# A vision tower's last three blocks: two routings at other places in the ending, and the last Exp in another method

## The chip, the cores and the metric

The kernel runs on one core of a Trainium2 chip. Its time is the device time of one execution in microseconds (us), and the median over several runs counts. The engines are TensorE (PE: matmuls; its weight loads are listed as PEld), VectorE (DVE), ScalarE (ACT) and GpSimd (POOL). SyncE (SP) issues most of the DMAs; ACT and POOL issue some from their own queues.

## The reference

A tokenizer, one layer with a recurrence ("retention") and an MLP, and a mixture of eight experts with the best two taken for each token, all in float32. Cut to what matters:

```python
# tokens: 16 samples of every 8, rfft over them, projected to D = 256
h = x_emb.reshape(B, V * N, -1)                  # 32 * 512 rows in all, 256 wide
# layer, on _layernorm(h)
q, k, v = n @ Wq.T + bq, n @ Wk.T + bk, n @ Wv.T + bv     # n = layernorm of the input
mem = decay * mem + k_t * v_t ;  ret_t = q_t * mem        # a scan over the tokens
x = x + ret
x = x + relu(layernorm(x) @ W1.T + b1) @ W2.T + b2        # W1: 1024 x 256
h = h + x
# experts, on tokens = layernorm(h)
logits = tokens @ router_w.T                              # 8 experts
rw, re = top_k(softmax(logits), 2);  rw = rw / rw.sum()
out = tokens + sum over e of combine[:, e] * (gelu(tokens @ w1[e] + b1[e]) @ w2[e] + b2[e])
h = h + out
```

## The kernel before

The 16,384 tokens are worked on in 32 blocks of 512 (`NB` = 32, the last is `NS` = 31), each as four tiles of 128 tokens on the partitions. Everything is fp32. A block passes through these steps, each a method of `Block`; the lines are those of the profile:

- `embed`: the tokenizer's products (L396) and its norm.
- `first_norm`, `retention` or `qkv` and `scan`: q, k, v from the transposed tokens (L339 on `wqkv_sb` in the ending), then on DVE `kv` L476, the scan `ks` L484 and `ret` L494. ACT makes a first `ks` (L474) and `z` (L438).
- `residual`: `ret` is turned back to tokens on PE (L608), added on DVE (L611) and normalized: statistics L263 and L264, a reciprocal square root by some ten small instructions L271 to L277, and `zz` L292.
- `features1`, `features2`: transposes of `zz` by DMA or on PE (L305), copied from PSUM on ACT (L306).
- `mlp_in(m)`, eight of them: one eighth of the first MLP product (L339 on `w1_sb`, `hT`), with relu on ACT (`aT`, L640). `mlp_out(u)`: the second product (L650, 32 matmuls each), added on DVE (L657), and after the second the norm that gives `tok` (L292).
- `rows`, `turn3`, `join3`, or `features3`: the tokens as rows in memory (ACT L698), and transposed for the router. `turn3` sends them through four transposing DMAs (L326, issued by SP) and `join3` puts the halves together (L332, on DVE for block 29); `features3` uses PE (L305) and ACT (L306).
- `logits` (PE L723), `choose` (DVE L747 to L764, then `ex`), `place` (PE L796, DVE L798 to L807, `weights` L774 to L777, then eight indirect DMAs of POOL, L819, which scatter the block's rows to `xbuf`, sorted by expert).
- `take(n, block, writes)` (DVE L864 to L932) plans the expert tiles: 256 rows of one expert each. `FULL` fixes how many tiles there are after each block. Block 29 gives four tiles, block 30 eighteen.

An expert tile (`Tile`) is handled in six steps. `load` (SP): weights `w` of 641.5 KB (L965), the rows transposed `xh` (L972) and their numbers `xg` (L975). `fetch` (L989): where `w` isn't loaded, it is copied from `bank`, on DVE and ACT in turn. `turn`: ACT makes `xT` (L995). `enter`: PE's first product (L1002) and gelu on ACT (L1010). `leave`: PE's second product (L1019). `sums`: DVE's L1031 to L1043, then two indirect DMAs of POOL which add the rows to `out` (L1048). `expert_halves` does one tile's enter and leave together with the other steps of the tiles ahead of it; `expert_step` runs it through. `bank` holds all eight experts' weights; `load_bank` issues its eight loads of 641.5 KB on ACT's queue (L944), one at each `next(weights)`. Before, only the tiles of block 30 take `w` from it. The last block isn't scattered: `combine` makes a weight for each token and expert, and `Expert` (PE L1081 and L1098, ACT L1088, DVE L1106 and L1112) computes all eight experts for its 512 tokens, between the tiles of block 30.

On SP, PE, DVE and ACT the order of the source is the order on the engine (`manual_schedule`); POOL's is left to a scheduler. So the order is written out by hand in a loop over blocks 0 to 30, in which three blocks are at work, and in an ending for the last three, called `old` (29), `mid` (30) and `last` (31). Pools bound how far an engine runs ahead: five `w`, six `xh`, twelve `xg`, four `y`, two `xT` and two `ge` buffers, and in PSUM two `mm` (for L305, L1002 and L1081) and three `tm` (for L608, L650, L723, L1019 and others).

Of the kernel before, what the change touches and what calls it, by code (L numbers as in the profile page):

```python
# [36 lines left out]
def vit_tower_kernel(  # L37
# [15 lines left out]
    nc = tc.nc  # L53
# [196 lines left out]
    def restore_weights():  # L250

        w = wqkv_sb.rearrange("p w k (m q) -> p w k m q", q=P)
        nc.vector.tensor_tensor(w[:, :, 0, 1], w[:, :, 1, 1], w[:, :, 0, 1], ALU.subtract)
# [96 lines left out]
    class Block:  # L350
# [381 lines left out]
        def choose(self):  # L732

            ps = self.lg
            shape = [P, TT, E]

            def wide(a):
                return a.unsqueeze(2).to_broadcast(shape)

            lg = small.tile(shape, F32, name="lg")  # L740
            top = small.tile([P, TT], F32, name="top")
            if self.i == NS:
                first_key = small.tile([P, TT], F32, name="first_key")
            else:
                first_key = self.row.bitcast(F32)[:, :, FIRST]
            turned = small.tile([P, TT, G], F32, name="turned_lg")
            nc.vector.transpose(turned.rearrange("p t g -> p (t g)"), ps.rearrange("p t g -> p (t g)"))  # L747
            nc.vector.tensor_reduce(top, turned[:, :, :E], AX.X, ALU.max)
            nc.vector.tensor_tensor(lg, turned[:, :, :E], wide(top), ALU.subtract)
            key = small.tile(shape, F32, name="key")  # L750
            self.oh = oh = small.tile([P, 2, TT, E], F32, name="oh")
            nc.vector.scalar_tensor_tensor(key, lg, 0.0, key0, ALU.is_equal, ALU.mult)
            nc.vector.tensor_reduce(first_key, key, AX.X, ALU.max)
            nc.vector.tensor_tensor(oh[:, 0], key, wide(first_key), ALU.is_equal)
            nc.vector.scalar_tensor_tensor(lg, oh[:, 0], -3.0e38, lg, ALU.mult, ALU.add)
            second = small.tile([P, TT], F32, name="second")
            nc.vector.tensor_reduce(second, lg, AX.X, ALU.max)
            nc.vector.tensor_tensor(key, lg, wide(second), ALU.is_equal)
            nc.vector.tensor_tensor(key, key, key0, ALU.mult)
            nc.vector.tensor_reduce(top, key, AX.X, ALU.max)  # L760
            nc.vector.tensor_tensor(oh[:, 1], key, wide(top), ALU.is_equal)
            dtype = F32 if self.i == NS else BF16
            self.both = small.tile(shape, dtype, name=f"both_{dtype.name}")
            nc.vector.tensor_tensor(self.both, oh[:, 0], oh[:, 1], ALU.add)  # L764
            self.ex = small.tile([P, TT], F32, name="ex")
            if self.i == NS:
                nc.scalar.activation(self.ex, second, AF.Exp)
            else:
                nc.gpsimd.tensor_tensor(self.ex, euler, second, ALU.pow)

# [7 lines left out]

        def combine(self):

            diff = small.tile([P, TT], F32, name="diff")
            second = small.tile([P, TT], F32, name="second")
            self.weights(diff, second)
            shape = [P, TT, E]
            self.share = self.both
            nc.vector.tensor_tensor(self.share, self.both, second.unsqueeze(2).to_broadcast(shape), ALU.mult)
            first = self.oh[:, 0]
            nc.vector.tensor_tensor(first, first, diff.unsqueeze(2).to_broadcast(shape), ALU.mult)
            nc.vector.tensor_tensor(self.share, self.share, first, ALU.add)
# [68 lines left out]
    def take(n, block, writes):  # L858
# [40 lines left out]
        expert = small.tile([P, KMAX], F32, name="expert")[:, :k]  # L899
        nc.vector.tensor_reduce(expert, past, AX.X, ALU.add)  # L900
        table = four.tile([P, 2, KMAX], I32, name="table")[:, :, :k]
        if block.i >= NS - 1:
            nc.vector.tensor_scalar(table[:, 0, :], expert, float(E - 1), None, ALU.min)
        else:
            nc.vector.tensor_scalar(table[:, 0, :], expert, float(P), float((E - 1) * P), ALU.mult, ALU.min)
# [47 lines left out]
    class Tile:  # L953
# [6 lines left out]
        def load(self):  # L960
            t = self.t
            self.w = five.tile([P, NW], F32, name="w")
            if self.block.i < NS - 1:
                wrow = nc.sync.value_load(self.table[:, 0, t : t + 1], min_val=0, max_val=(E - 1) * P)
                nc.sync.dma_start(out=self.w, in_=wex[bass.ds(wrow, P), :])  # L965

            def rows():
                row = nc.sync.value_load(self.table[:, 1, t : t + 1], min_val=0, max_val=ROWS - S)
                return xbuf[bass.ds(row, S), :]

            self.xh = six.tile([P, 2 * KD, S], U16, name="xh")
            read = nc.sync.dma_start(out=self.xh, in_=rows().bitcast(U16)[:, : 2 * D], transpose=True)  # L972
            unordered("rows", read, self.writes)
            self.xg = twelve.tile([P, 2, RW - D], I32, name="xg")
            read = nc.sync.dma_start(out=self.xg, in_=rows()[:, D:].rearrange("(c p) d -> p c d", p=P))  # L975
            unordered("rows", read, self.writes)
# [3 lines left out]
            return self.block.put == TT  # L980

        def fetch(self):
            if self.block.i >= NS - 1:

                assert len(loaded) == E
                t = self.t
                engine, copy = ((nc.vector, nc.vector.tensor_copy), (nc.scalar, nc.scalar.copy))[t % 2]
                e = engine.value_load(self.table[:, 0, t : t + 1], min_val=0, max_val=E - 1)
                copy(self.w.unsqueeze(1), bank[0][:, bass.ds(e, 1), :])  # L989
# [135 lines left out]
    def advance(what, upto):  # L1125
        while at[what] < min(upto, len(tiles)):
            if what == "load" and not tiles[at[what]].there():
                break
            getattr(tiles[at[what]], what)()
            at[what] += 1  # L1130

    def expert_halves(fetch=True, sums=True, load=True, turn=True):

        n = at["enter"]
        if load:
            advance("load", n + AHEAD)
        assert at["load"] >= min(n + 2, len(tiles))
        advance("turn", n + 1 + turn)
        advance("enter", n + 1)
        yield  # L1140
        advance("leave", n)
        if sums:
            advance("sums", n)
        if fetch:
            advance("fetch", n + AHEAD)

    def run(steps):
        for _ in steps:
            pass

    def expert_step(**how):
        run(expert_halves(**how))
# [2 lines left out]

    LEFT = 3

    def slot_halves(known, load=True, sums=True):

        if len(tiles) - at["enter"] > LEFT and at["enter"] + 2 <= known:  # L1160
            yield from expert_halves(load=load, sums=sums)

    def slot(known, load=True):
# [8 lines left out]
    with tc.manual_schedule(engines=MANUAL):  # L1172
# [3 lines left out]
        for i in range(NS):  # L1176
# [54 lines left out]
            if i:  # L1231
# [16 lines left out]
                    old.scatter(2, last_product[0])  # L1248
                next(qkv)
                advance("sums", at["leave"])  # L1250
                later = slot_halves(known, load=False)
                next(later, None)
                next(qkv)
                new.first_norm()
# [45 lines left out]
        old.join3(nc.vector.tensor_copy)  # L1300
        for m in range(KH):
            mid.mlp_in(m)
            if m in (1, 3, 5, 7):
                next(weights)
            if m == TT - 1:
                expert_step()
            if m == KH - 3:
                last.features1()
        next(weights)
        old.logits()  # L1310
        old.choose()
        expert_step()
        writes = old.place()
        next(weights)
        restore_weights()
        last.first_norm()
        last.retention(0)
        mid.mlp_out(0)
        next(weights)
        take(NS - 1, old, writes)  # L1320
        next(weights)
        mid.mlp_out(1)
        last.retention(1)
        beside = expert_halves(fetch=False)
        next(beside)
        mid.features3()
        mid.rows()
        advance("leave", at["enter"] - 1)
        mid.logits()
        mid.choose()  # L1330
        run(beside)
        expert_step(fetch=False, sums=False)
        writes = mid.place()
        advance("sums", at["leave"])
        expert_step(fetch=False, sums=False)
        last.residual()
        expert_step(fetch=False, sums=False)
        advance("sums", at["leave"])
        expert_step(fetch=False)
        take(NS, mid, writes)  # L1340

        last.features2()
        expert_step(turn=False)
        mid.store()
        last.sum_up()
        for m in range(KH):
            last.mlp_in(m)
            if m == TT - 1:
                advance("turn", at["enter"] + 1)
            if m == KH - 3:  # L1350
                expert_step()
# [109 lines left out]
```

## Time and profile before

| | us |
|---|---|
| median of five runs | 2114.7 |
| lowest and highest of them | 2111.08, 2118.17 |
| the profiled execution | 2115.45 |
| its span, first to last instruction | 2113.7 |
| PE busy in the span | 2080.0 |
| DVE busy | 1674.4 |
| ACT busy | 1099.6 |
| POOL busy | 885.0 |
| granted clock of PE, mean of the span | 0.994 of full |

A line of the timeline gives the start in us from the span's start, the duration, engine, source line, operation, output and inputs, and the number of instructions of the group; in brackets stand the idle time of the engine ahead of it and what ended that ("issue": nothing that the profile shows). In the waits of an engine a line names the waiting line, the releaser, the total in us, the number and the longest. In the table of windows each engine has its busy time and number of instructions in a stretch, then follow the granted PE clock, the DMA share and GB/s.

The ending begins near 1855 us of the span. In it stand, in this order, the first MLP product of block 30 (from 1862.8), block 29's router (L723 at 1880.94), the first q, k, v of the last block, both halves of `mlp_out` (from 1890.53), the second q, k, v, block 30's router (L723 at 1915.58), residual (L608 at 1923.30), the MLP of the last block with tiles between its parts, and from 2000 us on the experts.

### The profile page before, as it was taken

What the parts mean: (1) busy time and instruction counts of PE and PEld (TensorE: products, weight loads), DVE (VectorE), ACT (ScalarE), POOL (GpSimd) and SP (SyncE); (2) the same over time, 40 slices, a digit from 0 to 9 for tenths busy, and PEclk for the clock granted to TensorE, in tenths of its full rate; (3) what the DMA queues carried; (4) which work ended last, traced back from release to release, by engine and by line L of the source; (5) the groups of instructions that cost most, each with busy time, mean ns of one, the idle gap of its engine ahead of it and who ended that gap; (6) DMA issues with size and microseconds to landing.
All of it is one profiled execution on the core that took longest, in us unless ns stands there. A gap on an engine that the chain in (4) does not pass through costs nothing.

```text
span 2113.7 us, 30454 instructions
## 1 busy us (share of the span) xinstructions
PE 2080.0 (98%) x9042; PEld 1577.6 (75%) x9042; DVE 1674.4 (79%) x5179; ACT 1099.6 (52%) x1966; POOL 885.0 (42%) x768
## 2 busy tenths in 40 slices
PE   8999999999999999999999999999999999998999
PEld 6777677777777777777777777787777787675776
DVE  6778888888888888888888888888888888767445
ACT  2344455655545665555556555455665545544443
POOL 1032234444444444444444444444444444534444
PEclk9999999999999999999999999999999999999999
DMA  4031256766676676667667766676776667686553
GB/s 142 2 123 64 80 135 139 160 142 122 140 157 147 157 159 137 130 138 160 153 148 160 149 124 137 157 155 144 163 159 122 132 150 161 141 224 141 90 70 49
DMA packets 424519, 283.21 MB, mean 134 GB/s; under 512 B 355104, under 2 KB 391072, under 8 KB 420256
## 3 DMA queue, kind: packets, MB, share of 16 engines
q1 hardware_dynamic: 373424, 208.35, 42.4%
q0 software_dynamic: 49632, 67.39, 17.5%
q10 hardware_dynamic: 1296, 5.52, 0.7%
q8 instruction: 71, 1.16, 0.2%
q14 instruction: 96, 0.79, 0.1%
HBM read 118.36 MB, written 86.52 MB: 97 GB/s over the span
## 4 chain that ended last, share of the span: by engine, by line
PE 75%; DVE 10%; DMA 5%; ACT 5%; issue 2%; SPq 2%; POOL 1%; ACTq 0%; DVEq 0%; POOLq 0%
PE tm L650 17%; PE sums L339 14%; PE tm L396 9%; PE sums L524 9%; PE mm L1002 9%; PE tm L1019 8%; DMA turned<-planes 3%; DVE st L263 2%; SPq L326 2%; PE mm L540 1%; ACT planes L318 1%; PE tm L1098 1%; PE mm L1081 1%; PE mm L539 1%; ACT tokT L332 1%
## 5 line engine op out<-in xcount | busy, mean ns | idle before, releaser
L1048 POOL DMA_INDIRECT out<-y,xg x226 | 365.7, 1618 | 426.4 <-DVE y L1038 220.4
L650 PE MATMUL tm<-w_sb,aT 128*128 128x256 f32 x2048 | 454.7, 380 | 0.0
L339 PE MATMUL sums<-hT,w_sb 128*128 128x512 f32 x1024 | 451.1, 593 | 0.3 <-ACT aT L640 0.3
L650 PEld LDWEIGHTS tm<-w_sb,aT 128*128 128x128 f32 x2048 | 386.7, 190 | 57.2 <-DVE z L611 4.9
L819 POOL DMA_INDIRECT xbuf<-row,to x248 | 258.8, 1044 | 293.9 <-DVE ks L560 170.6
L339 PEld LDWEIGHTS sums<-hT,w_sb 128*128 128x128 f32 x1024 | 193.5, 190 | 218.2 <-issue 200.9
L396 PE MATMUL tm<-wu,xv 128*128 128x256 f32 x1280 | 282.5, 379 | 0.0
L318 ACT COPY planes<-zz 128x1024 uint16<-128x1024 uint16 x100 | 99.3, 1040 | 342.1 <-DVE zz L292 342.1
L396 PEld LDWEIGHTS tm<-wu,xv 128*128 128x128 f32 x1280 | 242.7, 190 | 32.7
L1002 PE MATMUL mm<-xT,w 128*128 128x256 f32 x1048 | 252.3, 384 | 5.2 <-ACT xT L995 3.4
L1019 PE MATMUL tm<-w,ge 128*128 128x256 f32 x1048 | 253.9, 385 | 0.0
L1002 PEld LDWEIGHTS mm<-xT,w 128*128 128x128 f32 x1048 | 201.1, 193 | 47.9 <-issue 15.6
L1019 PEld LDWEIGHTS tm<-w,ge 128*128 128x128 f32 x1048 | 196.5, 191 | 31.7 <-issue 2.9
L640 ACT ACTIVATE aT<-sums,vec 128x512 f32<-128x512 f32 x256 | 166.9, 691 | 59.8 <-PE sums L339 57.8
L995 ACT COPY xT<-xh 128x512 uint16<-128x512 uint16 x262 | 182.1, 767 | 20.2 <-DMA xh<-xbuf 17.2
L1010 ACT ACTIVATE ge<-mm,w 128x256 f32<-128x256 f32 x262 | 109.7, 474 | 140.6 <-PE mm L1002 84.7
L283 POOL TENSOR_SCALAR rstd<-mv 128x4 f32<-128x4 f32 x62 | 41.9, 676 | 333.2 <-DVE mv L264 296.7
L1036 DVE TENSOR_TENSOR y<-tm,w 128x512 f32<-128x512 f32 x131 | 90.5, 691 | 99.0 <-PE tm L1019 98.5
L332 ACT COPY hT<-turned 128x512 uint16<-128x512 uint16 x100 | 66.2, 761 | 80.4 <-DMA turned<-planes 80.4
L263 DVE BATCH_NORM_STATS2 st<-h 128x6 f32<-128x256 f32 x256 | 104.9, 410 | 3.3
L524 PE MATMUL sums<-hT,wqkv_sb 128*128 128x256 f32 x360 | 107.1, 379 | 0.0
L371 DVE TENSOR_TENSOR xv<-xb 128x512 f32<-128x512 f32 x160 | 104.3, 684 | 3.5 <-DMA xb<-in_x 3.5
(224 smaller groups left out, 3081.0 us busy)
## 6 DMA issues: line engine op xcount, KB each, us to landing
w<-in_wex SPq DMA_DIRECT2D x113, 641.5 KB
xb<-in_x SPq DMA_DIRECT2D x32, 1040.0 KB
out<-h SPq DMA_DIRECT2D x31, 512.0 KB
bank<-in_wex ACTq DMA_DIRECT2D x8, 641.5 KB
xbuf<-row,to POOLq DMA_INDIRECT x248
out<-y,xg POOLq DMA_INDIRECT x226
xh<-xbuf SPq DMA_TRANSPOSE x131
xg<-xbuf SPq DMA_DIRECT2D x131, 4.0 KB
```

Of the source, the lines that this page charges most:

```text
L263: nc.vector.bn_stats(self.st[:, t, :], src[:, t, :])
L318: nc.scalar.copy(planes[:, :, i * D : (i + 1) * D], half)
L339: nc.tensor.matmul(ps, lhsT=w[:, k, ts(m, P)], rhs=rhs[:, k, :], start=k == 0, stop=k == KD - 1)
L396: nc.tensor.matmul(ps[:, n, :], lhsT=xv[:, i, j, :], rhs=wu[:, i, j, :], start=j == 0, stop=j == J - 1)
L524: nc.tensor.matmul(g[:, n, :], lhsT=lhsT, rhs=rhs, start=False, stop=True, skip_group_check=True)
L640: nc.scalar.activation(self.aT[:, m, :], ps, AF.Relu, bias=vec[:, MB1 + m : MB1 + m + 1])
L650: last_product[0] = nc.tensor.matmul(ps[:, i, :], lhsT=self.aT[:, k, ts(u * 2 + i, P)], rhs=w2_sb[:, k, :], start=k == 0, stop=k == KH - 1,)
L819: write = nc.gpsimd.indirect_dma_start(out=xbuf, out_offset=bass.IndirectOffsetOnAxis(ap=self.to[:, c, t : t + 1], axis=0), in_=self.row[: ...
L995: nc.scalar.copy(halves[:, :, :, 1 - i], self.xh[:, i * KD : (i + 1) * KD, :])
L1002: nc.tensor.matmul(ps[:, m, :], lhsT=self.w[:, k * D + m * P : k * D + (m + 1) * P], rhs=self.xT[:, k, :], start=k == 0, stop=k == KD - 1,)
L1019: last_product[0] = nc.tensor.matmul(ps[:, c, :], lhsT=self.ge[:, k, ts(c, P)], rhs=w[:, (2 + k) * D : (3 + k) * D], start=k == 0, stop=k ...
L1048: add = nc.gpsimd.indirect_dma_start(out=out, out_offset=bass.IndirectOffsetOnAxis(ap=number[:, c, :], axis=0), in_=y[:, c, :], in_offset= ...
```

## The change

Four things are edited.

- The last block's Exp is called in `combine` instead of `choose`.
- The tiles of block 29 take `w` from `bank` as those of block 30 do: three conditions on `NS - 1` become `NS - 2`, in `take` (the table then holds the number of an expert instead of a row), `load` and `fetch`.
- The ending is put in another order. Block 29's `logits` and `choose` come inside block 30's first MLP product, after m = 4, and its `place` right after m = 7; two expert steps there are gone from their places. Both halves of `mlp_out` of block 30 come next, with block 29's `take` between them, and the first q, k, v product of the last block after them. Block 30's router follows with one tile and a half around it, then its `place`, `take(NS)`, the second q, k, v product, two expert steps, `residual`, two expert steps and `features2`. Block 30's store and the last block's `sum_up` come after m = 1 of the last `mlp_in`, and the expert step which skips a `turn` after m = 3. `restore_weights` and the bank's loads are at other places.
- `slot_halves` takes a parameter `left` whose value is everywhere the constant that was there.

```diff
             if self.i == NS:
-                nc.scalar.activation(self.ex, second, AF.Exp)
+                self.second = second
...
         def combine(self):
+            nc.scalar.activation(self.ex, self.second, AF.Exp)
...
-        if block.i >= NS - 1:
+        if block.i >= NS - 2:
             nc.vector.tensor_scalar(table[:, 0, :], expert, float(E - 1), None, ALU.min)
...
-            if self.block.i < NS - 1:
+            if self.block.i < NS - 2:
                 wrow = nc.sync.value_load(...)
                 nc.sync.dma_start(out=self.w, in_=wex[bass.ds(wrow, P), :])
...
         for m in range(KH):
             mid.mlp_in(m)
-            if m in (1, 3, 5, 7):
+            if m in (1, 4, 7):
                 next(weights)
             if m == TT - 1:
-                expert_step()
-            if m == KH - 3:
                 last.features1()
+                restore_weights()
+            if m == KH - 4:
+                old.logits()
+                old.choose()
+        writes = old.place()
+        last.first_norm()
+        out_steps = mid.mlp_out_steps(0)
+        next(out_steps)
         next(weights)
-        old.logits()
-        old.choose()
-        expert_step()
-        writes = old.place()
-        next(weights)
-        restore_weights()
-        last.first_norm()
-        last.retention(0)
-        mid.mlp_out(0)
+        run(out_steps)
         next(weights)
         take(NS - 1, old, writes)
+        out_steps = mid.mlp_out_steps(1)
+        next(out_steps)
         next(weights)
-        mid.mlp_out(1)
-        last.retention(1)
-        beside = expert_halves(fetch=False)
-        next(beside)
+        run(out_steps)
+        next(weights)
+        last.retention(0)
+        next(weights)
+        beside = expert_halves()
         mid.features3()
         mid.rows()
-        advance("leave", at["enter"] - 1)
+        next(beside)
         mid.logits()
+        run(beside)
         mid.choose()
-        run(beside)
-        expert_step(fetch=False, sums=False)
+        expert_step()
         writes = mid.place()
-        advance("sums", at["leave"])
-        expert_step(fetch=False, sums=False)
+        take(NS, mid, writes)
+        last.retention(1)
+        expert_step()
+        expert_step()
         last.residual()
-        expert_step(fetch=False, sums=False)
-        advance("sums", at["leave"])
-        expert_step(fetch=False)
-        take(NS, mid, writes)
+        expert_step()
+        expert_step()
         last.features2()
-        expert_step(turn=False)
-        mid.store()
-        last.sum_up()
         for m in range(KH):
             last.mlp_in(m)
+            if m == 1:
+                mid.store()
+                last.sum_up()
             if m == TT - 1:
+                expert_step(turn=False)
                 advance("turn", at["enter"] + 1)
```

## The prediction

> **What bounds the kernel now.** I read the page first, for the engine with no slack:
>
> ```profile
> span 2113.7 us, 30454 instructions
> PE 2080.0 (98%) x9042; PEld 1577.6 (75%) x9042; DVE 1674.4 (79%) x5179; ACT 1099.6 (52%) x1966; POOL 885.0 (42%) x768
> ```
>
> PE leaves 33.7 us, and the change keeps its instructions and only reorders them in the last 250 us. So the question is which PE gaps of the ending close, and which open. Second, the waits of PE from 1860 to 2022 us:
>
> ```profile
> PE mm L305 <- issue: 4.9, 1, 4.9
> PE mm L1002 <- ACT xT L995: 3.4, 1, 3.4
> PE mm L1002 <- ACT hT L306: 1.2, 1, 1.2
> PE tm L608 <- DVE y L1036: 0.7, 1, 0.7
> ```
>
> With 0.96 (L305 for tok), 0.49 (L1002) and 0.24 (L723) unshown, the ending loses 12.0 us to waits. Third, the windows table, whose column after POOL is the granted PE clock:
>
> ```profile
> 1819.00:1826.00 7.00, 4.85 (x15) 3.66 (x14) 6.17 (x21) 4.86 (x11) 4.49 (x3) 0.76 1.07 286
> 1933.00:1946.50 13.50, 7.33 (x25) 5.65 (x24) 9.01 (x40) 4.40 (x10) 7.83 (x6) 0.75 0.94 195
> 2000.00:2014.00 14.00, 10.56 (x41) 8.35 (x41) 7.13 (x30) 8.14 (x12) 7.25 (x5) 0.76 0.51 65
> ```
>
> Every longer gap is paid twice: it is followed by some 3.4 to 7 us at half clock. Fourth, PE's timeline shows that price (start, duration, idle before):
>
> ```profile
> 1821.74 0.73 PE L539 MATMUL mm<-hT,wqkv_sb 128*128 128x256 f32 x2 [2.15 <-ACT ge L1010]
> 1938.29 1.11 PE L305 MATMUL mm<-ident,zz 128*128 128x128 f32 x4 [4.92 <-issue]
> 1940.64 3.78 PE L1002 MATMUL mm<-xT,w 128*128 128x256 f32 x8 [1.25 <-ACT hT L306]
> 2007.41 3.78 PE L1002 MATMUL mm<-xT,w 128*128 128x256 f32 x8 [3.44 <-ACT xT L995]
> 2010.98 3.10 PE L1019 MATMUL tm<-w,ge 128*128 128x256 f32 x8
> ```
>
> A tile's L1002 group takes 1.73 us on the chain elsewhere, here 3.78.
>
> **The change, part by part.** The yardstick is the profiled execution: 2115.45 us, a span of 2113.7 with 1.75 around it, and 0.75 above the median 2114.7. Less than 0.2%, 4.2 us, can't be told from no change.
>
> *Exp of the last block, from choose to combine.* In ACT's timeline it stands ahead of a tile's xT:
>
> ```profile
> 2004.58 1.28 ACT L767 ACT_TABLE_LOAD   x1 [4.74 <-DVE second L757]
> 2005.87 0.21 ACT L767 ACTIVATE ex<-second 128x4 f32<-128x4 f32 x1
> 2005.98 1.37 ACT L995 COPY xT<-xh 128x512 uint16<-128x512 uint16 x2
> 2007.37 1.28 ACT L1010 ACT_TABLE_LOAD   x1
> ```
>
> ACT idles 4.74 us for `second`, and PE waits for the xT behind it. Moved, Exp follows that xT and two tiles' gelu, so L1002 starts on time: 3.44 us gone, and with it the half clock after it, L1002 3.78-1.73=2.05 and L1019 2.90-1.73=1.17 (chain of waits): 6.66 together. Both table loads stay. Behind the Exp on ACT are now another xT (1.37), the second load (1.28) and two kv of 0.69. Walked from L723's end at 2000.25: L1002, L1019, L1002, L1019 (1.73 each) and L1081 (3.43) keep PE until 2010.6, the next L1019 until 2012.3. ACT ends the second gelu near 2006.3, its bank copy (1.26) and Exp near 2009, xT 2010.4, load 2011.7, first kv 2012.4. The next L1002 needs the mm buffer which that kv reads: 0.1 to 0.8 us late, I take 0.3. Sum here -6.4.
>
> The Trainium skill speaks against it: "ScalarE: Activation LUTs", What ACT_TABLE_LOAD costs, adds a drain of 1.38 us to each load of 1.28. In the rows above ACTIVATE starts 1.29 us after the load, with no such gap. By the page, kv would come up to 2.8 us later and the gain here would be 3.6 at the least.
>
> *Block 29's four tiles take w from the bank.* Four loads of 641.5 KB leave SP's queue; one of them had held the xh behind it until 1921.94, for which ACT waited 5.10 us and PE 0.49. In their place come two DVE copies (0.83) and two ACT copies (1.26). They are covered by PE's tiles, but one DVE copy stands directly ahead of residual's L611; it is in the walk below. All ACT copies wait for all eight bank loads; before these were out by 1896.5, before any of the copies is due (1920).
>
> *The reordered stretch, 1862 to 1946.* Before it held waits of 0.96+0.71+0.49+4.92+1.25=8.33 us, and half clock of 0.5 (L305) + 2.05 (L1002) + 0.42 (L1019: 2.15): 11.3. I walk the new order from PE free at 1862.8.
>
> (a) L723 of block 29 now comes after mlp_in m=4. Four m of 1.72, L305 0.87, one m: PE is there at 1872.3. Its input:
>
> ```profile
> 1873.22 1.46 DVE L332 COPY tokT<-turned 128x512 uint16<-128x512 uint16 x4 [1.97 <-DMA turned<-row]
> ```
>
> It ends at 1874.68, and its transposes (SP, issued 1863.01 to 1868.14) aren't moved. New wait 2.4 us, between 1.3 (the DMAs less crowded, as the second bank load comes later) and 2.6. Before, two expert steps covered it; they are what was taken out.
>
> (b) m5-m7, L796 (its `both` 3.0 after L723, by 1878.7), mlp_out's L650 x64 (13.8) and retention's first twelve L339 (5.17): no wait until 1899.5. Behind L650 the chain L657 to tok takes 4.8 (1907.37 to 1912.18 before), which retention covers within 0.2: the 0.96 goes.
>
> (c) L305; then L1002 waits 0.5 for the tokT copies on ACT; L723, L1019, L1002, L1019, and L796 at 1908.5, where `both` is ready at 1907.6 on DVE (ret 3.7 after tok, sums 1.7, choose 3.0). Then retention 5.17 and two tiles (6.9): PE stands before L608 at 1920.7. DVE: place 2.7, take 5.5 (it was at 1941, in PE's stall, and is now ahead of ret), ret 3.7 gives 1921.1, and the sums freeing L608's second tm 1.1 later: 1.0 us wait, where 0.71 was.
>
> (d) Residual: after L608 PE has two tiles, until 1929.6. DVE has two sums (3.4), the copy (0.83) and then L611 to zz, 7.4 (1925.12 to 1932.54 before): zz at 1933.1. New wait 3.5 us for L305, then hT 1.25 as before. This is what is late next: the zz chain, for which the old order had the same two tiles' cover.
>
> New waits: 2.4+0.5+1.0+3.5+1.25=8.65. Half clock: (d) is as long as what before cost 3.0 to 3.2, (a) as long as the 2.15 at 1821.74, after which the window stood at 0.76. I take 2.5 together (between 0 and 5.1). So 11.15 against 11.3: this stretch gives nothing.
>
> The clock rule of the Trainium skill ("TensorE: Matmul & The Clock Gate", HAM oscillation) tells to keep PE gaps under some 3.4 us. By it (a) would cost no clock and only (d) some. But the 2.15 us gap was followed by half clock, so the row decides.
>
> (e) Signals. Before, while POOL issued 12 indirect DMAs in a row,
>
> ```profile
> 1937.39 0.84 ACT L1010 ACTIVATE ge<-mm,w 128x256 f32<-128x256 f32 x2 [3.90 <-issue]
> 1937.23 1.55 POOL L1048 DMA_INDIRECT out<-y,xg  x1 [0.30 <-issue]
> ```
>
> L1010 started 6.1 us after its L1002 had ended at 1931.2, and L657 at 1907.37 3.0 after L650 (1904.34). Block 30's burst moves to about 1912-1925, over the tiles at L608. Between 0 (bursts of six in the main loop show none; (d) hides the first 3.5) and 2.6. I take 1.0.
>
> (f) Queues passed. SP: block 30's store (512 KB) waits ACT's L683, now behind mlp_in m=1, near 1941 instead of 1947.3, so the xh queued behind it go out earlier, not later: 0. ACT: the bank loads slip to m=1, 4, 7, four behind L438 and one behind L474; each waits only for transfers issued by 1880, and what stands behind (L474, tokT) is due at 1898 and later: 0, and up to 3 if they crowd as the last two did (9.36 us on that queue). POOL: block 29's scatter (1896.68 before) starts near 1883, its reads follow it: 0.
>
> The sum: -6.66+0.3-11.3+11.15+1.0=-5.5. 2115.45-5.5=2109.95, less 0.75: 2109.2 as a median.
>
> **Rivals.** *No change that can be told.* Exp gains its 6.4, but the stretch returns some of it: (a) and (d) each get a full half-clock window of 1.7 more than I took on average, or (d) is 5 us since DVE is the later engine. 2109.2+2.5=2111.7, up to 2115. For: the new order leaves DVE chains of 11 us (sums, copy, residual) against 7 us of PE. Against: these chains are sums of measured rows, none is unseen.
>
> *Slower: late signals.* The place is the burst of block 30's eight L819 with L1048 on both sides, now from place to residual. If its lateness hits twice, L657 by 3.0 in the first burst (tok, no cover left: +2.8) and ACT's L1010 by 6.1 in the second ahead of the zz chain, which depends on the DVE sums of that tile (+6.1), with a further slow window (1.7): -5.5-1.0+10.6=+4.1 on the run, a median of 2118.8 and up to 2122. It decides from 9 us of lateness on. For: both rows above. Against: the first burst now starts near 1883, under 13.8 us of L650 with nothing due, and ends by 1897.
>
> *Larger gain.* L1010's lateness came from the four w loads, which leave: (d) falls to 1.5 and the clock stays: 2109.2-2-2.5-1=2103.7.
>
> **How the numbers follow.** The forecast (2105.5 to 2110.5) has 0.38, the larger gain 0.16, no change 0.28, slower 0.18. Faster by over 0.2% (under 2110.5) is 0.54; within 0.2% (to 2118.9) 0.3, taking some of the slower rival; slower 0.16. The range goes from 2102 (larger gain, with (a) at its low bound) to 2120 (into the slower rival).
>
> **What would show it.** Right: no table load between L723 and the second L1002, and no wait of L1002 for xT near 2004; a wait of 1.3 to 2.6 us at L723 near 1872 with DVE's L332 as releaser; one of 2 to 5 at L305 (zz) near 1930 with DVE as releaser; both slow stretches after 1930 down to one. Wrong: L657 or L1010 starting over 3 us after their PE groups; an L1081 or L1002 waiting over 1 us for kv; or a wait at L305 under 1 us.

## The result and the profile after

The changed kernel takes 2116.62 us as a median of 24 runs, the kernel before 2115.14 of 44; the ratio is 1.0004, with a 95% interval of 0.9998 to 1.0011. So it is no change that can be told. 2109.2 was forecast. The profiled execution has a span of 2113.5 us (before 2113.7).

What makes this worth reading is that PE did nearly what the prediction says. The waits of PE after, from 1800 us on:

```profile
PE tm L1020 <- ACT ge L1011: 4.3, 1, 4.3
PE mm L539 <- issue: 2.5, 1, 2.5
PE tm L723 <- DVE tokT L332: 2.1, 2, 1.8
PE tm L797 <- DVE oh L761: 1.1, 1, 1.1
```

The wait of 3.4 us for xT behind the Exp is gone, the new one of L723 is there at 2.1, and near the L305 of residual one long wait is left, that of L1020 for gelu. (Lines after the edit in `combine` stand one higher, those from `mlp_in` of the ending on up to two.) PE's last line, before and then after:

```profile
2105.32 3.62 PE L1098 MATMUL tm<-bank,ret 128*128 128x256 f32 x16
```
```profile
2100.19 3.62 PE L1099 MATMUL tm<-bank,ret 128*128 128x256 f32 x16
```

PE ends 5.1 us earlier, and 6.0 earlier counted from the first product of the ending (1863.67 after, 1862.79 before). The span is 0.2 shorter. The chain of waits shows who ends last instead; its last pieces before, then after (start, duration, what):

```profile
2102.03 6.93 PE tm L1098 x32
2108.96 0.02 issue
2108.98 0.70 DVE zz L1106
2109.69 0.03 issue
2109.71 0.48 DVE h L1112
2110.19 0.40 DVEq L1457
```
```profile
2099.69 1.61 POOL out L1049
2101.29 0.30 issue
2101.60 4.05 DMA out<-y,known
...
2106.43 1.57 POOL out L1049
2108.00 1.86 POOLq L1459
```

Before, the last expert's products, DVE's sum and a store end the program. After, it is POOL: each expert tile's two scatter-adds wait until the former tile's have landed. POOL's timeline has the reason, before and then after:

```profile
1881.78 1.55 POOL L1048 DMA_INDIRECT out<-y,xg  x1 [6.69 <-DMA out<-y,xg]
1892.93 1.60 POOL L1048 DMA_INDIRECT out<-y,xg  x1 [6.54 <-DVE ret L494]
2104.78 1.66 POOL L1048 DMA_INDIRECT out<-y,known  x1 [0.30 <-issue]
```
```profile
1909.16 1.64 POOL L1049 DMA_INDIRECT out<-y,xg  x1 [14.36 <-DVE y L1039]
1931.54 1.60 POOL L1049 DMA_INDIRECT out<-y,xg  x1 [0.30 <-DVE st L263]
2108.30 1.56 POOL L1049 DMA_INDIRECT out<-y,known  x1 [0.30 <-issue]
```

The two expert steps that were taken out of block 30's first product had their scatter-adds at 1881.78 and 1892.93. Now no pair is issued between 1874.14 and 1909.16, POOL idles 14.4 us at the end of that stretch, and from 1931.54 on 27 pairs stand in one chain, a pair every 6.73 us ((2106.43-1931.54)/26): two issues of 1.55 to 1.9, two gaps of 0.3 and some 3 us for landing. Before, 25 pairs from 1943.24 came every 6.65 us and ended 3.5 us earlier. Two paths lead to the end: the end of PE's last product plus 4.8 us (2113.7-2108.94, before), and the end of POOL's last issue plus 3.6 us (2113.5-2109.86, after). The later of them sets it:

| | PE's path | POOL's path |
|---|---|---|
| before | 2113.7 | 2110.0 |
| after | 2108.6 | 2113.5 |

### The profile page after: what moved, and what is told of

It reads as the page before. It is cut to its first block, busy times and chain, and to the rows that moved or that the text cites. A ratio compares the mean times of both kernels' runs of the same rounds, so it can differ in the third digit from the quotient of the medians.

```text
span 2113.5 us, 30446 instructions
## 1 busy us (share of the span) xinstructions
PE 2075.8 (98%) x9042; PEld 1573.5 (74%) x9042; DVE 1676.4 (79%) x5181; ACT 1102.5 (52%) x1968; POOL 885.4 (42%) x768
## 3 DMA queue, kind: packets, MB, share of 16 engines
q8 instruction: 71, 1.16, 0.2%
## 4 chain that ended last, share of the span: by engine, by line
PE 77%; DVE 8%; ACT 5%; DMA 4%; issue 2%; POOL 2%; SPq 1%; POOLq 0%; ACTq 0%; another core or an unknown queue 0%; DVEq 0%
PE tm L650 18%; PE sums L339 14%; PE tm L396 10%; PE sums L524 9%; PE mm L1003 8%; PE tm L1020 8%; DMA turned<-planes 3%; PE mm L540 1%; ACT planes L318 1%; DVE st L263 1%; PE mm L539 1%; ACT tokT L332 1%; PE mm L1082 1%; PE tm L1099 1%; SPq L326 1%
## 5 line engine op out<-in xcount | busy, mean ns | idle before, releaser
L1020 PE MATMUL tm<-w,ge 128*128 128x256 f32 x1048 | 253.8, 385 | 4.3 <-ACT ge L1011 4.3
L1003 PE MATMUL mm<-xT,w 128*128 128x256 f32 x1048 | 247.9, 379 | 0.3 <-ACT tokT L306 0.2
L1003 PEld LDWEIGHTS mm<-xT,w 128*128 128x128 f32 x1048 | 198.7, 190 | 41.3 <-issue 14.8
L1020 PEld LDWEIGHTS tm<-w,ge 128*128 128x128 f32 x1048 | 195.8, 191 | 36.2 <-ACT ge L1011 4.7
L1011 ACT ACTIVATE ge<-mm,w 128x256 f32<-128x256 f32 x262 | 110.1, 476 | 152.8 <-PE mm L1003 97.9
L1037 DVE TENSOR_TENSOR y<-tm,w 128x512 f32<-128x512 f32 x131 | 90.6, 691 | 99.0 <-PE tm L1020 98.7
L332 ACT COPY hT<-turned 128x512 uint16<-128x512 uint16 x100 | 66.2, 761 | 82.2 <-DMA turned<-planes 82.2
L332 ACT COPY tokT<-turned 128x512 uint16<-128x512 uint16 x116 | 76.5, 760 | 59.8 <-DMA turned<-row 59.8
```

The costliest lines, as they stand in the source:

```text
L332: copy(to[:, 1 - i], self.turned[:, :, i, k, :])
L1003: nc.tensor.matmul(ps[:, m, :], lhsT=self.w[:, k * D + m * P : k * D + (m + 1) * P], rhs=self.xT[:, k, :], start=k == 0, stop=k == KD - 1,)
L1020: last_product[0] = nc.tensor.matmul(ps[:, c, :], lhsT=self.ge[:, k, ts(c, P)], rhs=w[:, (2 + k) * D : (3 + k) * D], start=k == 0, stop=k ...
```

## The experiments

Theory A is these two paths. Theory B is the prediction's own yardstick: PE alone sets the end.

**The Exp alone**, in the kernel before.

```diff
-                nc.scalar.activation(self.ex, second, AF.Exp)      # choose
+                self.second = second
...
+            nc.scalar.activation(self.ex, self.second, AF.Exp)     # combine
```

> The kernel before with the Exp alone moved to combine. Theory A (scatter-add chain): the span ends with the later of two paths, PE's last product plus 4.8 us, and POOL's chain of scatter-adds (L1048, 25 pairs from 1943 us at 6.65 us each) plus 3.6 us. Before, these end at 2113.7 and 2110.0, so the move may bring 3.7 us at most: about 2111.4 us as a median, ratio 0.9983, with PE's last product at about 2102.3 and POOL last. Theory B (the sum of the prediction, PE alone sets the end): 6.4 us, 2108.7 us, ratio 0.9970.

2115.75 us, ratio 0.9995 (0.9982 to 1.0007). PE's last product ends at 2102.4, as expected, and the chain of waits ends on POOL:

```profile
2106.60 1.56 POOL out L1049
2108.16 1.86 POOLq L1458
```

B's 0.9970 lies outside the interval. A's 0.9983 is at its edge: I had POOL's chain at 6.65 us a pair, and in this execution it came every 6.81 ((2106.60-1943.09)/24) and ended the span at 2113.8. The spare of 3.7 us on POOL that the profile before shows is that of one execution.

**The changed kernel without the Exp's move.**

> The changed kernel with the Exp back in choose. Theory A: PE's path becomes 6.7 us longer, from 2108.6 to 2115.3 in the span, POOL's stays at 2113.5: 1.8 us slower than the changed kernel, ratio to before 1.0013. Theory B: 6.4 us slower than the changed kernel, ratio to before 1.0035.

2120.16 us, ratio 1.0012 (1.0002 to 1.0022): A's figure, and B's 1.0035 is outside. But the number agrees with A better than the profile does. PE's path is at 2115.9 there, near A's 2115.3, yet POOL's chain was 4.5 us later than A had it (27 pairs from 1933.38, one every 6.83 us) and set the end, at 2118.3.

**A shorter chain on POOL**, in the changed kernel, in the kernel before, and in the one with the Exp alone.

```diff
+            if self.block.i == NS - 1 and self.t == FULL[NS] - FULL[NS - 1] - 1:
+                return
             before = added[-2:] + [self.block.stored]
```

> The changed kernel without the scatter-adds (and their sums on DVE) of the last of block 30's eighteen tiles, whose rows are left out of the output; its matmuls stay. Theory A: POOL's chain is one pair of 6.7 us shorter and PE's path becomes the end: 4.9 us faster than the changed kernel, ratio to before 0.998. Theory B: no change, as PE works as long as before: ratio 1.000.

> The kernel before without the scatter-adds of the last of block 30's tiles, whose rows are left out of the output. Theory A: PE's path set the end there, POOL's chain had 3.7 us to spare: no change, ratio 1.000 (at the least 0.9985, where the chain is slow in some executions). If the chain alone set the end before, 0.997.

> The kernel before with the Exp in combine and without the scatter-adds of the last of block 30's tiles, whose rows are left out of the output. Theory A: the chain on POOL is a pair shorter, so the whole 6.4 us of PE show: ratio to before 0.997. Theory B: as with the Exp alone, 0.9995.

The edit leaves out the two scatter-adds alone; the tile's sums on DVE still run (L1037 counts 131 as before). In the changed kernel 2111.06 us, ratio 0.9970 (0.9959 to 0.9982), with PE's products as before. In the kernel before 2114.88, 0.9995 (0.9985 to 1.0005). With the Exp alone 2109.97, 0.9971 (0.9959 to 0.9982), while the Exp without this edit brought 0.9995. The same two scatter-adds are worth nothing where PE's path is the longer one, and as much as the whole move where it isn't. The chain of waits of the first of the three ends on PE and DVE again:

```profile
2096.63 6.94 PE tm L1101 x32
2103.57 0.02 issue
2103.59 0.70 DVE zz L1109
```

This settles A against B. It also shows that the Exp's 6.4 us were there on PE (0.9971 is 6.1 us).

**Tiles given back.** One after m = 3; then a second between the halves of `mlp_out`.

```diff
             if m == TT - 1:
+                expert_step()
                 last.features1()
...
         take(NS - 1, old, writes)
+        expert_step()                      # with two only
```

> The changed kernel with one expert step given back to block 30's first product, after m = 3. Theory A: one pair of scatter-adds moves into POOL's idle time near 1885, the chain ends 6.7 us earlier, and the 2.1 us wait of L723 is covered: the span ends near 2107, ratio to before 0.997. Theory B: only the 2.1 us wait is gone: ratio to before 0.9994.

> As the run with one tile given back, and a second tile between the halves of block 30's mlp_out. Theory A: POOL's chain is 25 pairs from about 1935 us and ends 6.7 us earlier than with one (near 2099.5), so that PE's path sets the end again: PE's last product near 2105, span near 2109.8, ratio to before 0.998. Rival: the second tile's scatter-adds queue behind block 29's eight scatters on POOL and the chain starts no earlier: no gain over one tile, 0.9989.

One: 2114.19 us, 0.9989 (0.9978 to 1.0000). The wait of L723 for L332 was covered, as both theories have it, and POOL ended at 2108.1 instead of 2109.9, 1.8 us earlier and not 6.7, so that A's 0.997 lies outside the interval, and B's 0.9994 can't be told from what was measured: one pair fewer stood in the chain, but it began at 1935.44, where the changed kernel's began at 1931.54, and came every 6.76 us. Others of PE's waits opened (1.8 for tok, 1.8 for zz, 1.7 for hT). My figure was too high on both paths. Two: 2108.01 us, 0.9962 (0.9950 to 0.9974), the lowest ratio here. POOL's last pair starts at 2096.46, so PE sets the end, as A has it; its last product ends at 2101.1, 3.9 us earlier than expected, and the time is below A's 0.998. It beats both kernels.

**The row of scatters.** Block 30's eight scatters issued in pairs behind tiles; in the changed kernel, and with two tiles given back.

```diff
-        writes = mid.place()
+        writes = mid.place(at_once=False)
+        mid.scatter(1, last_product[0])
...                                         # 2, 3 and 4 behind expert steps
```

> The changed kernel with block 30's eight scatters in four pairs, each behind a tile's products; PE's order is the same. In the changed kernel L1011 started 7.2 us after its L1003 and PE waited 4.3 us for it, beside a row of eight scatters and two scatter-adds. Theory C (the row delays PE's signals): that wait falls under 1 us, and PE's last product comes 4 to 6 us earlier. Theory D (another cause): the wait stays over 2 us. The time stays at the changed kernel's by theory A, ratio 1.000, as POOL's chain is as long.

> As the run with two tiles given back, with block 30's eight scatters in four pairs, each behind a tile's products, instead of in one row. PE's order is the same. Theory C (a row of 10 to 12 indirect DMAs of POOL delays the signals): no wait of PE for gelu or L305 over 1 us between 1915 and 1945, and no half clock there; PE's last product 3 to 5 us earlier than with two tiles, ratio to before 0.996. Theory D (the lateness has another cause): as with two tiles, 0.998.

The parts 2, 3 and 4 come behind the first, third and fourth of the steps in the changed kernel, and behind the first three with two tiles.

In the changed kernel 2117.78 us, 1.0008 (0.9997 to 1.0018). The wait of PE for gelu is gone. The trace's semaphore records say what was late: in the changed kernel, PE's signals to ACT for the groups that end at 1928.40, 1930.13 and 1931.86 come together at 1935.52 to 1935.71, and with the scatters in pairs each comes within 0.03 us of its group's end. But L305 waits 3.5 us for zz in its place, so PE ends no earlier; C's second half fell, and A's ratio held. With two tiles 2109.96, 0.9971 (0.9960 to 0.9982), no better than without the edit, which had no such wait to begin with though its row of scatters was whole; PE's last product ended at 2105.1 instead of 2101.1, where C has it earlier. So the row isn't enough to make L1011 late, and zz was due about as late anyway. What delays PE's signals stays open.

**Better cover**: the second tile behind the first q, k, v product, and `take` behind residual; then a third tile between the halves too.

```diff
         last.retention(0)
         next(weights)
+        expert_step()
...
-        take(NS, mid, writes)
         last.retention(1)
...
         last.residual()
+        take(NS, mid, writes)
```

> As with two tiles given back, but the second one behind the last block's first q, k, v product, where PE waited 1.4 us for tok, and block 30's take moved behind residual, so that it no longer stands ahead of ret on DVE (PE waited 2.4 us for ret). Theory A: POOL's chain is no longer than with two tiles and PE's path sets the end, so each PE wait that closes counts: tok 1.4 and ret 2.4 and the two stretches of half clock behind them (1.8 each) go, ratio to before 0.993 to 0.994. Rival: the DVE chain for zz (two sums, the bank copy, L611 to zz) is late instead, and PE waits there: 0.996 as with two tiles.

> Three tiles given back (after m = 3, between the halves of mlp_out, and behind the last block's first q, k, v product) and block 30's take behind residual: PE's order of the run in which PE's last product came at 2097.6 but POOL's chain ended at 2110.7. Theory A: the third tile takes one more pair off the chain (6.7 us), so that POOL ends near 2104 and PE's path near 2102.5 to 2104 in the span: ratio to before 0.994 to 0.995. Rival: tiles of block 30 are now due sooner than their rows have come (xh), PE waits for xT, and the time is that of two tiles, 0.996.

With two tiles 2108.75 us, 0.9968 (0.9955 to 0.9980). PE's waits for tok and ret closed as expected, and its last product ended at 2097.6, 3.5 us earlier than with the other two tiles, but POOL ended last, and so it didn't count; the expected 0.993 to 0.994 was missed:

```profile
2098.05 4.55 DMA out<-y,known
...
2103.38 1.57 POOL out L1049
2104.95 1.87 POOLq L1461
```

The second tile came behind retention, and so its scatter-adds at 1911.30 instead of 1895.29; the last chain has 25 pairs as with the other two tiles, but starts at 1941.67 instead of 1935.47. (This execution, of 2112.48 us, is 3.7 above the median.) Three: 2112.09, 0.9991 (0.9980 to 1.0002), outside what both theories expected. POOL's chain was short, its last pair at 2097.43, but PE waited 7.8 us, not for xh as the rival had it. PE's and ACT's timelines:

```profile
1950.67 8.78 PE L339 MATMUL sums<-hT,w_sb 128*128 128x512 f32 x16 [7.81 <-ACT hT L306]
```
```profile
1948.87 1.26 ACT L990 COPY w<-bank 128x1283 f32 x1 [8.67 <-DVE y L1037]
1950.04 1.06 ACT L306 COPY hT<-mm 128x512 f32<-128x512 f32 x2
```

ACT's copy of a bank weight stands ahead of hT and waits for the w buffer, which DVE's sums free; those now stood behind `take`, 5.8 us of DVE after zz.

**w by DMA for block 29's tiles**, with two tiles given back (the three conditions `NS - 2` back to `NS - 1`).

> As with two tiles given back, but block 29's four tiles load w by DMA as before the change instead of copying it from the bank. Theory A': the w loads again hold the xh behind them in SP's queue until a w buffer comes free, ACT waits for xh and PE for xT: 2 to 5 us slower than with two tiles, ratio to before 0.997 to 0.9985. Rival: with tiles done earlier the w buffers come free in time, and the four copies on DVE and ACT are gone: 0.996.

2113.89 us, 0.9986 (0.9973 to 0.9998), against 0.9962 with the bank's copies: with two tiles given back, this part of the change is worth some 5 us, at the upper end of what was expected. How it comes about is not what was expected, as far as one execution shows, and that one was the slowest of its ten (2118.29). PE doesn't wait for xT; L608 waits 5.3 us and L305 2.6. Even so PE's path would have ended at 2111.5 (2106.7+4.8). POOL set the end, at 2116.5: its last 25 pairs started at 1944.79, not at 1935.47.

L608's wait came over POOL too. `ex` (L769) stood behind a scatter-add that began at 1922.04 after 13.7 us of idle time, where with the bank's copies it began at 1914.03, and DVE waited 4.9 us for `ex`. By the semaphore records the pair before it, issued from 1904.84, had landed only at 1920.55 (with the bank's copies one issued from 1895.29 had landed at 1903.34). From 1905 to 1921 the DMA column of the windows stands at 1.16, with the bank's copies at 0.48. That the w loads made this landing late is argued and not shown. SP did stand still ahead of w loads, as the theory has it, but the long stop, from 1924.95 to 1936.97, came too late to have held this scatter-add back.

**The two paths over all runs.** In each of the fourteen profiled executions, those before and after included, the later of the two paths meets the span within 0.4 us. PE's is the later in seven of them, POOL's in the other seven.

## Why the prediction was right and wrong

The median was in the range of 2102 to 2120, 7.4 us above the 2109.2 forecast, and no change had been given 0.3. That was luck: the reason is not the one that this rival gave, as the reordered stretch did not give back what the Exp gained. On PE the prediction was nearly right; it had the wrong path to the end.

- **The step that failed is the yardstick.** "PE leaves 33.7 us ... So the question is which PE gaps of the ending close": this holds only while PE's path is the longest. The profile before had POOL's as close as 3.7 us behind, in its timeline and in the waits of L1048 for the DMA of the former pair, and I didn't put the two ends side by side. In (f), POOL's part was set at 0 with block 29's scatter alone in view. The two expert steps had been counted as cover for L723 ("they are what was taken out"), their scatter-adds not at all. Their move to the end of the queue is worth +3.5 us on POOL's end, and with that -5.1 on PE's became -0.2 on the span. Without the last pair of scatter-adds the changed kernel took 0.9970 of the time before: there the gain on PE shows.
- **Exp: right.** The wait for xT and the half clock after it went, and the next tile's product came 0.2 us late (0.3 was said). The loads' drain that the Trainium skill adds ("ScalarE: Activation LUTs", What ACT_TABLE_LOAD costs) isn't in the trace after either; ACTIVATE follows the load at once:

```profile
2005.56 1.28 ACT L781 ACT_TABLE_LOAD   x1
2006.85 0.21 ACT L781 ACTIVATE ex<-second 128x4 f32<-128x4 f32 x1
2008.35 1.28 ACT L1089 ACT_TABLE_LOAD   x1
2009.65 1.27 ACT L1089 ACTIVATE kv<-mm,bank 128x512 f32<-128x512 f32 x2
```

- **(a) L723: right**, 2.1 us against 2.4, with no half clock behind it.
- **(b), (c): nearly.** tok 0.6 (0.2), tokT 0.2 (0.5), L608 0.7 (1.0); L796 waited 1.1 us, where I had it ready 0.9 us ahead.
- **(d), (e): the sum near, the terms not.** No wait of 3.5 us for zz, none for hT, and one of 4.3 for gelu: L1011 started at 1935.59, 7.2 us after L1003's end, where I took 1.0 beyond cover. zz came at 1938.2, not 1933.1, so that PE would have waited there next. 4.3 stand against 3.5+1.25+1.0. Two of the prediction's own signs of being wrong came here: gelu over 3 us behind its products, and no wait at L305 for zz.
- **Half clock:** some 1.8 us (L1020 3.38 for 1.89, L305 1.38 for 1.04 in the timeline) against 2.5. In all the stretch cost 10.8 us of waits and half clock, where 11.15 and 1.0 for the signals were said.

## What to carry to other kernels

An engine at 98% is the bound only as long as no other chain ends near it: before summing the waits of one engine, put down when each engine's last work ends and what follows it, in more than one execution, and take the smallest distance as the most that can be gained. A step taken out of one place is work on every queue that it feeds; a queue that works one item at a time, with a landing between, gives back a place left empty one period later at its end. Here the cure was to give the steps back, not to close more waits.

## What the hardware showed besides

A wait of the same length was followed by half clock in one execution and not in another. Behind the Exp, L1002 waited 3.44 us before and ran at 3.78; in the kernel before without the two scatter-adds it waited 3.49 and ran at full clock at once. PE's timeline, and the row of the windows which had a clock of 0.76 before and has 1.00 here:

```profile
2007.30 1.99 PE L1002 MATMUL mm<-xT,w 128*128 128x256 f32 x8 [3.49 <-ACT xT L995]
2009.13 1.95 PE L1019 MATMUL tm<-w,ge 128*128 128x256 f32 x8
```
```profile
2000.00:2014.00 14.00, 10.51 (x48) 7.42 (x41) 9.51 (x37) 8.74 (x13) 6.44 (x5) 1.00 0.45 57
```

With the Exp back in the changed kernel a wait of 2.62 did bring it (L1019 3.21 us for 1.89 behind it). So "every longer gap is paid twice" was too firm: the second price, here between 0 and some 3.4 us (14 us at 0.76 of the clock), depends on more than the gap's length, and belongs into the range. What else it depends on, no run here shows.
